# Twenty-four loads moved from ScalarE's queue to GpSimd's in a two-block convolution kernel

## The chip, the cores and the metric

The kernel runs on one core of a Trainium2 chip. The metric is the device time of one execution in microseconds (us). TensorE (PE) multiplies matrices, its weight loads are shown as PEld, VectorE is DVE, ScalarE is ACT, GpSimd is POOL, SyncE is SP. SP, ACT and POOL can each ask for DMA transfers; the instruction that asks is called the issue here.

## What is computed

Two residual blocks on x of shape (8, 96, 96, 192), all in float32:

```
x = x + L0(groupnorm(x))
x = x + L1(groupnorm(x))
...
# L1, the ConvNeXt-like block
y = conv_general_dilated(x, dw_kernel 7x7, SAME, feature_group_count=192) + dw_bias
y = (y - mean_c) * rsqrt(var_c + 1e-6) * ln_gamma + ln_beta
y = gelu(y @ w0 + b0)          # 192 -> 768
y = (y @ w1 + b1) * gamma      # 768 -> 192
```

L0 projects 192 channels to 384, convolves them 3x3 per channel, adds four running averages along rows and columns, normalizes and projects back. Only L1's 7x7 convolution and what surrounds it matter here.

## The kernel before

The work is staged. Stages A to C compute block L0 and leave its result x1 in DRAM as X1_d. Stage D is the 7x7 convolution; stage E ("the last pass") takes the convolution's output back from DRAM (Y_d), normalizes each pixel over the channels, runs the two dense layers and stores the result.

**Stage D** has 32 steps: two halves of the batch (four images each) times 16 groups of 12 channels. A step is one call pattern of conv_d: six sub-steps c, each with two PSUM banks, 24 matmuls (L1337) and two evictions on ScalarE (L1347) that write the step's output tile yo. The first N1 = 19 steps, numbered n = 0 to 18, are the stage's "own steps": they run by themselves in the loop that the diff touches (L1622). The other 13 are later mixed into stage E in slots. In each own step the program order is, engine by engine:

- POOL: load_raw(n + 2) asks for the rows of the step after next, six transfers of 384 KB (L926). Each waits until VectorE has scaled the rows two steps earlier (L960) out of the same buffer.
- SP: load_band(n + 2), one transfer of 624 KB (L936), then store_d(n - 1), the output of the step before: for each of two channel groups one transfer of 810 KB (L1364) and two of 27 KB (L1368, L1369).
- DVE: scale_steps(n + 1) normalizes the rows of the next step into xin (24 instructions, L960), and copies its band to the other half of the partitions (L964).
- PE and ACT: conv_d(n, c) for c = 0 to 5. Before its first eviction, yo must be free: yo has one buffer for even and one for odd steps, so the stores of step n - 2 must have landed.

The order of the instructions is as the program has it (manual_schedule); nothing reorders them afterwards. Eight PSUM banks stand between TensorE and ScalarE, so TensorE can be four sub-steps ahead.

**Tile 0 of the last pass.** Stage E works through tiles; load_y(n) gathers one from Y_d into two SBUF tiles ya and yb. It gives a list of steps: begin (allocates, L1387), then for each image b and for b = NH (the remainder) eight pieces q. A large piece (L1398) reads 32 rows by 5 channel groups in runs of 384 bytes, 60 KB in all, from one part of Y_d, called a chunk: five groups of six channels, that is, the output of two and a half convolution steps. A small piece (L1404) is 16 KB. Since Y_d is filled in the order of the groups, tile 0's large pieces can be asked for while stage D is still running. main_y lists which, by step: chunks 0 and 1 in step 12 (NI = 16, so NI - 4), chunks 2 and 3 in step 13, and chunk 4 (twice) in step 14. These are 8 pieces in each of three steps; they are asked for two after each of the first four sub-steps. The rest, chunk 5 and the small pieces, follows in step 16 from SP and POOL (rest_y), and tile 1 in step 17.

Each piece is a lambda whose engine is an argument with a default; main_y's loop passes the engine.

After the loop, VectorE sums tile 0 over the channels (L1486, norm_steps_e) and the chain to the first dense layer (L1549) begins.

## Time and profile before

| what | value |
|---|---|
| median of 3 runs | 5425.03 us (5417.93 to 5442.97) |
| the profiled execution | 5427.67 us |
| its span, first to last instruction | 5425.9 us |
| TensorE busy | 5255.3 us, 97% |
| VectorE, ScalarE, GpSimd busy | 64%, 48%, 44% |
| own steps of stage D in the span | about 2590 to 2907 us |
| large pieces asked for by ACT | 24, from 2798.8 to 2852.6 us |

Times inside the profile count from the span's start. A line of the waits reads: waiter and its line <- whom it waited for: total us, times, longest us. A line of a timeline reads: start, duration, engine, line, operation, tiles, count, and in brackets the idle time before it with what ended it. A queue line of the DMA view reads: queue and kind: packets, MB, share of the time of 16 DMA engines. q0 is POOL's queue, q1 SP's, q10 ACT's.

### The profile page before, as it was taken

How to read it: one execution, taken by the hardware profiler on the slowest of the kernel's cores; microseconds unless marked ns; L12 is line 12 of the kernel's file. 1: busy time of each engine (PE TensorE's matmuls, PEld its weight loads, DVE VectorE, ACT ScalarE, POOL GpSimd, SP SyncE). 2: the span in 40 equal slices, each digit the busy share in tenths (PEclk: the TensorE clock that was granted, in tenths of full speed). 3: DMA queues.
4: the chain of work that ended last, by engine and by line, in shares of the span. 5: the costliest groups of instructions: out<-in, count | busy, mean ns of one | idle time of the engine just before them, and what ended most of it. 6: DMA issues, size and time to landing. Idle time of an engine off the chain costs nothing. (4 is left out here: it accounts for less than half of the span.)

```text
span 5425.9 us, 107893 instructions
## 1 busy us (share of the span) xinstructions
PE 5255.3 (97%) x42206; PEld 3342.3 (62%) x42206; DVE 3460.8 (64%) x6722; ACT 2578.2 (48%) x5765; POOL 2386.7 (44%) x2105
## 2 busy tenths in 40 slices
PE   6999999999999999999787999999999999999999
PEld 4666643333333799999444666666666667666667
DVE  6555539999999555555556555555566666666654
ACT  2444446777777566565434444454433333323332
POOL 1111118888888555555324222233233333333332
PEclk9999979999999999999898999999999999999999
DMA  7999868999999799899997455545433233332331
GB/s 221 286 286 276 251 181 235 244 246 242 247 241 250 226 306 308 276 303 311 293 299 205 119 137 136 132 120 138 108 80 78 80 81 84 87 93 80 81 78 41
DMA packets 788107, 1015.33 MB, mean 187 GB/s; under 512 B 326199, under 2 KB 662272, under 8 KB 785552
## 3 DMA queue, kind: packets, MB, share of 16 engines
q1 hardware_dynamic: 671432, 633.30, 44.2%
q0 software_dynamic: 86128, 335.43, 18.7%
q10 hardware_dynamic: 30040, 39.72, 3.2%
q8 instruction: 334, 5.47, 0.4%
q14 instruction: 173, 1.42, 0.1%
HBM read 603.70 MB, written 420.03 MB: 189 GB/s over the span
## 5 line engine op out<-in xcount | busy, mean ns | idle before, releaser
L1579 PEld LDWEIGHTS hp<-w1g,g 128*128 128x128 f32 x6912 | 1117.9, 190 | 140.7 <-issue 82.8
L1579 PE MATMUL hp<-w1g,g 128*128 128x192 f32 x6912 | 1174.9, 329 | 0.0
L1568 ACT ACTIVATE g<-hp,b0g 128x512 f32<-128x512 f32 x864 | 518.9, 691 | 1216.1 <-PE hp L1559 1192.9
L1598 POOL DMA_DIRECT2D out_dram<-xo x288 | 211.3, 734 | 1532.5 <-DVE xo L1590 1461.6
L1590 DVE TENSOR_TENSOR xo<-hp,r 128x384 f32<-128x384 f32 x288 | 229.0, 795 | 995.2 <-PE hp L1579 994.9
L1549 PE MATMUL hp<-yT,w0w 128*128 128x512 f32 x1728 | 779.3, 597 | 19.9 <-DVE yT L1534 19.3
L1141 PE MATMUL po<-wc,mt 128*128 128x193 f32 x3456 | 666.4, 328 | 7.5 <-DVE x1c L1175 7.3
L688 PE MATMUL pl<-pin,band 34*32 34x380 f32 (+1 forms) x13824 | 639.0, 496 | 6.4 <-DMA pin<-PL_d 4.2
L775 POOL TENSOR_TENSOR mo<-mo,z 128x768 f32<-128x768 f32 x285 | 593.9, 2084 | 5.7 <-ACT mo L713 1.6
L1141 PEld LDWEIGHTS po<-wc,mt 128*128 128x128 f32 x3456 | 556.0, 192 | 8.9 <-DVE x1c L1175 8.3
L1549 PEld LDWEIGHTS hp<-yT,w0w 128*128 128x128 f32 x1728 | 321.2, 190 | 380.3 <-issue 350.2
L721 DVE TENSOR_TENSOR_SCAN z<-decay,loc 128x768 f32<-128x768 f32 x288 | 505.9, 1757 | 63.7 <-ACT loc L697 34.6
L730 DVE TENSOR_TENSOR_SCAN z<-decay,z 128x768 f32<-128x768 f32 x288 | 498.3, 1730 | 0.0
L1337 PE MATMUL hp<-xin,band 63*64 63x372 f32 (+1 forms) x4608 | 417.9, 498 | 69.3 <-ACT yo L1347 37.3
L688 PEld LDWEIGHTS pl<-pin,band 34*32 34x32 f32 x13824 | 233.7, 108 | 393.5 <-issue 390.9
L709 PE MATMUL pa<-loc,mix 128*32 128x384 f32 x3456 | 439.3, 500 | 0.0
L712 PE MATMUL pa<-last,down 96*32 96x384 f32 x1152 | 434.2, 500 | 0.9 <-ACT mo L713 0.9
L1559 PE MATMUL hp<-yT,w0w 64*128 64x512 f32 x1728 | 419.5, 611 | 0.0
L1513 POOL TENSOR_TENSOR rs<-tot,neg_half 32x32 f32<-32x32 f32 x72 | 394.7, 5481 | 48.2 <-DVE tot L1511 47.4
L1347 ACT ACTIVATE yo<-hp,dwb 128x384 f32<-128x384 f32 x384 | 196.5, 583 | 430.5 <-PE hp L1337 268.1
L697 ACT COPY loc<-pl 128x384 f32<-128x384 f32 x576 | 248.0, 482 | 313.1 <-PE pl L688 313.1
L395 PE MATMUL pm<-xT,win 128*128 128x384 f32 x1152 | 391.9, 490 | 0.0
(159 smaller groups left out, 7261.6 us busy)
## 6 DMA issues: line engine op xcount, KB each, us to landing
P<-po POOLq DMA_DIRECT2D x96, 1152.0 KB, 9.4
pin<-P SPq DMA_DIRECT2D x190, 576.0 KB
mt<-M SPq DMA_DIRECT2D x192, 384.0 KB
xq<-in_x_dram SPq DMA_DIRECT2D x96, 576.0 KB
xr<-in_x_dram SPq DMA_DIRECT2D x192, 288.0 KB
X<-x1c SPq DMA_DIRECT2D x144, 384.0 KB
out_dram<-xo POOLq DMA_DIRECT2D x288, 192.0 KB, 2.4
r<-X SPq DMA_DIRECT2D x35, 1536.0 KB
```

Source lines behind the costliest of these rows:

```text
L688: nc.tensor.matmul(pls[g][at * RB : (at + 1) * RB, :, lo:hi], band[rows, c, kh, :], pin[rows, c, :, NJ - 1 - j, lo + kh - 1 : hi + kh - 1] ...
L709: nc.tensor.matmul(pa[at], mix[:, i, at], loc[:, q], start=True, stop=True)
L712: nc.tensor.matmul(pa[at], down[:, to], last[:, q], start=True, stop=True)
L721: nc.vector.tensor_tensor_scan(zf, decay_f, loc.rearrange("p q n -> p (q n)"), 0.0, ALU.mult, ALU.add)
L730: nc.vector.tensor_tensor_scan(zr, decay_f, zr, 0.0, ALU.mult, ALU.add)
L775: eng.tensor_tensor(m, m, z, ALU.add)
L1141: nc.tensor.matmul(po, mt[:, m, j * 128 : (j + 1) * 128], wc[:, m], start=(m == 0), stop=(m == NC - 1),)
L1337: nc.tensor.matmul(pys[g][k * 64 : (k + 1) * 64, :, lo:hi], band[rows, k * GS + c, d * ZS : d * ZS + 64], xin[rows, :, :, k * GS + c, lo + ...
L1549: nc.tensor.matmul(hps[m, q], w0w[:, 0, m * 128 : (m + 1) * 128], yT[:, 2 * q], start=True, stop=False,)
L1559: nc.tensor.matmul(hps[m, q], w0w[p, 1, m * 128 : (m + 1) * 128], yT[p, 1], start=False, stop=True,)
L1568: nc.scalar.activation(g[:, m, q], hps[m, q], AF.Gelu, bias=b0g[:, m : m + 1], scale=1.0)
L1579: nc.tensor.matmul(po[:, q], g[:, m, q, k * 128 : (k + 1) * 128], w1g[:, m], start=(m == 0), stop=(m == NE - 1),)
```

## The change

In the loop of the own steps the large pieces of main_y are given to GpSimd in place of ScalarE. Nothing else is edited: the same 24 pieces, in the same steps, at the same places in the program. On ACT they stood between the evictions of a step; on POOL they stand behind the six row loads that load_raw(n + 2) has put there earlier in the same step, and ahead of those of load_raw(n + 3).

```
                 for c in range(GS):
                     conv_d(n, c)
                     for step in main_y.get(n, [])[2 * c : 2 * c + 2]:
-                        step(nc.scalar)
+                        step(nc.gpsimd)
                     if c == 2:
                         for step in between:
                             step()
```

More of the change, by code (lines that the diff above doesn't have):

```diff
@@ L1649, in conv_blocks_kernel @@
                     for step in main_y.get(n, [])[2 * c : 2 * c + 2]:
-                        step(nc.scalar)
+                        step(nc.gpsimd)
                     if c == 2:
```

## The prediction

> **What bounds the kernel now.** I went from the page to the stretch that the edit touches. The slices come first, each 135.6 us wide; the edit lies in the 21st and 22nd.

> ```profile
> PE   6999999999999999999787999999999999999999
> DMA  7999868999999799899997455545433233332331
> GB/s 221 286 286 276 251 181 235 244 246 242 247 241 250 226 306 308 276 303 311 293 299 205 119 137 136 132 120 138 108 80 78 80 81 84 87 93 80 81 78 41
> ```

> TensorE is full nearly everywhere (9) and falls to 7 and 8 only in slices 20 to 22. From slice 23 on it is full again, so a microsecond saved in the own steps of the 7x7 convolution is one saved at the end: all that follows hangs on that convolution's results and is TensorE-bound. Next, who waited for whom between 2590 and 2920 us (total, times, longest):

> ```profile
> POOL raw L926 <- DVE xin L960: 169.2, 38, 28.1
> ACT yo L1347 <- DMA Y<-yo: 126.5, 15, 28.4
> ...
> ACT yo L1347 <- DMA ya<-Y: 24.3, 7, 6.2
> ...
> ACT yo L1347 <- DMA yb<-Y: 6.1, 1, 6.1
> ```

> The evictions wait mostly for the stores of the same yo buffer two steps earlier, not for TensorE. Only 24.3 + 6.1 = 30.4 us are waits behind the pieces. The timeline of ScalarE at step 12, the first with pieces (start, duration, [idle before]):

> ```profile
> 2798.74 0.58 ACT L1347 ACTIVATE yo<-hp,dwb 128x384 f32<-128x384 f32 x1 [11.97 <-DMA Y<-yo]
> ...
> 2802.32 5.43 ACTq L1398 DMA_DIRECT2D ya<-Y  x2
> 2807.80 1.05 ACT L1347 ACTIVATE yo<-hp,dwb 128x384 f32<-128x384 f32 x2 [6.09 <-DMA ya<-Y]
> 2809.97 3.50 ACTq L1398 DMA_DIRECT2D ya<-Y  x2
> 2813.53 1.99 ACT L1347 ACTIVATE yo<-hp,dwb 128x384 f32<-128x384 f32 x4 [4.67 <-DMA ya<-Y]
> 2821.70 0.58 ACT L1347 ACTIVATE yo<-hp,dwb 128x384 f32<-128x384 f32 x1 [6.18 <-DMA Y<-yo]
> ```

> The twelve evictions of step 12 last from 2798.74 to 2815.5, 16.8 us; those of step 11 ran from 2778.31 to 2786.76, 8.5 us. The same timeline gives the starts: step 3 at 2664.05 and step 11 at 2778.31, so 14.28 us a step; then 2798.74, 2821.70, 2841.87, 2864.85 (step 15), 2875.89, 2885.79. The three steps with pieces take 23.0, 20.2 and 23.0 us. SyncE's timeline shows a second effect:

> ```profile
> 2786.79 0.33 SPq L1364 DMA_DIRECT2D Y<-yo  x1
> 2797.94 0.26 SPq L1368 DMA_DIRECT2D Y<-yo  x1
> 2798.65 0.26 SPq L1369 DMA_DIRECT2D Y<-yo  x1
> 2807.90 0.33 SPq L1364 DMA_DIRECT2D Y<-yo  x1
> ```

> ```profile
> q0 software_dynamic: 5208, 18.34, 50.5%
> q1 hardware_dynamic: 5674, 18.58, 49.9%
> ```

> ```profile
> q0 software_dynamic: 2443, 8.59, 48.8%
> q1 hardware_dynamic: 2117, 6.96, 35.2%
> q10 hardware_dynamic: 4209, 1.47, 10.2%
> ```

> The ordinary steps are bound by the DMA engines: 100.4% busy. In steps 12 to 14 they are still 94% busy. That limits what the edit can give.

> [...]

> **The change part by part.**

> *Removed from ScalarE:* 24 issues, and the 30.4 us of waits with them. The evictions of steps 12 to 14 should last 8.5 us each instead of 16.8, 12.9 (2821.70 to 2834.55) and 14.7 (2841.87 to 2856.55): 18.9 us in sum, on the path only as far as the stores can follow.

> *Removed from the shared semaphores:* the pattern of SP returns to that of steps 3 to 11, and the late store (about 10 us in each of three steps) goes. It overlaps the item above, so the two aren't added.

> *What is late next: the DMA engines.* The bytes stay. At the rates of steps 3 to 11 (18.34 MB in 57.6 us, 18.58 in 56.9: 0.318 and 0.326 MB/us) the traffic of 2798 to 2865 needs 8.59/0.318 + 6.96/0.326 + 6.8 (the pieces' own 10.2% of 67 us) = 55.2 us. That is 11.8 us less than the 67 taken. If the slow rate came from the mixture itself, only the idle share comes back: 5.2% of 67, 3.5 us. So 3.5 to 12 us by step 15. Steps 15 to 17 ran 82% busy, and rows that come later fill them: -3 to +6 us. I take 8 + 3 = 11 us.

> *Added to GpSimd:* eight issues a step at 0.57 us (its median on L1398), 4.6 us beside rows of 4.4 us in steps of 20 us. Their issue time is hidden by GpSimd's wait for L960 (169.2 us in all). The waits that they bring are not free: after six rows, the last six of eight pieces each look back to one of these rows, so the last piece waits until the rows have landed, and the next step's rows stand behind it. A row lands after

> ```profile
> raw<-X POOLq DMA_DIRECT2D x18, 384.0 KB, 12.9
> ```

> 12.9 us (median, steps 12 to 14), 13.1 us in ordinary steps, 18.2 us at most. With L for this and 4.6 us for issuing six rows, a turn of GpSimd is 5.6 + L, some 19 us. Rows 15 then start at about 2798 (rows 14 went out by 2784, plus L) instead of 2788.45, rows 17 two turns later, and rows 18, whose third looks back to the first of rows 17, are complete at 2798 + 2(5.6 + L) + 0.6 + L + 2.5 + L = 2812 + 4L. Before, VectorE took rows 18 at 2883.43. With L = 13.5 they are there at 2866, 17 us earlier: an 11 us gain fits. The break-even is L = 17.9. The chunk of step 14's pieces holds output of step 12; its store, issued by about 2808, must have landed. GpSimd reaches them near 2820: a cost of 0, at most 3 us. Data for tile 0 come earlier or as late as before, well ahead of VectorE's first sum at 2892.15.

> Sum: 5427.67 us (the profiled execution; span 5425.9) - 11 = 5416.7. It stood 2.6 us above the median of 5425.03, so I forecast **5414 us**.

> **The rivals.**
> *Full recovery.* Steps 12 to 14 fall to 14.28 us plus 2.3 us each for the pieces (6.8/3): 49.7 instead of 66.1 us, 16.4 us, and step 12 and the tail give some 8 more. For it: the late store vanishes completely. Against it: 94% busy engines. 5425 - 24 = 5401.
> *Hidden anyway.* ScalarE, free of the pieces, waits at L1347 for the store instead, since only 3.5 us of the engines' time was idle, and later rows take those back. For it: 126.5 us of that wait already. 5425 - 2 = 5423.
> *Slower: rows behind pieces.* GpSimd's turn becomes the bound. From L = 17.9 us each further microsecond costs four. The most seen is 18.2. With the stores busy without pause and half the rate left for the rows, six of them (2.36 MB) take 2.36/0.163 = 14.5 us, so it needs a further disturbance[...]. At L = 21: 4 x 3.1 = 12 us, 5437; at L = 25 it would be 28 us, 5453.

> **How the numbers follow.** The forecast 0.58, full recovery 0.14, hidden 0.19, slower 0.09. A measurement of this kernel can tell about 0.5% (27 us) from no change; the runs shown spread from 5417.93 to 5442.97. Faster by more needs the upper end of full recovery: 0.06. Slower by more needs L near 25: 0.03. Within: 0.91. The range 5399 to 5430 takes in the 3.5 to 18 us of the forecast, most of full recovery, all of "hidden", and leaves out most of "slower".

> **What would show it.** Right: no idle of L1347 put down to ya or yb, twelve evictions in 8.5 us in steps 12 to 14, the second L1364 of a step a few us after its first, DMA near 100% and some 330 GB/s from 2798 on, starts of steps 13 to 15 some 15 to 18 us apart, TensorE's last L1337 of step 18 some 11 us before 2907.1. Wrong: VectorE (L960) waiting for raw in steps 15 to 17 says GpSimd's turn is the bound; starts still 20 us or more apart with L1347 waiting for Y<-yo says the transfers were.

## The result and the profile after

The changed kernel takes 5410.21 us (median of 21 runs, 5404.86 to 5434.75); the kernel before, on the same chip, 5428.17 us (21 runs). The ratio is 0.9971, 95% interval 0.9962 to 0.9979: some 16 us less, a small gain, but one that the runs can tell from nothing. The forecast was 5414 us.

A caution on the trace: the profiled execution of the changed kernel took 5428.47 us, 18 us above its median; its own steps began late (step 3 at 2666.6 us instead of 2664.05, step 11 at 2783.07 instead of 2778.31) ahead of the first moved piece at 2790.78, in code that the edit doesn't touch, and step 12 began at 2806.05 instead of 2798.74. So I compare stretches inside the stage, not spans, and give the same stretches of the repeat run (label after_again, 5412.05 us) beside them.

The slices of the changed kernel hardly differ from those of before: in the 21st the DMA engines stay at 9, in the 22nd they go from 7 to 8; a few us in a slice of 135.7 us hardly show.

```profile
PE   6999999999999999999787999999999999999999
DMA  7999869999999799899998455545433233332331
GB/s 221 285 286 277 251 183 239 247 240 244 246 243 246 230 306 308 273 301 312 282 308 206 119 137 135 131 120 138 108 79 78 80 81 85 87 92 80 81 78 41
```

The waits of the changed kernel between 2590 and 2920 us (total, times, longest):

```profile
POOL raw L926 <- DVE xin L960: 115.9, 27, 28.1
ACT yo L1347 <- DMA Y<-yo: 112.2, 11, 30.2
...
DVE xin L960 <- DMA raw<-X: 26.4, 8, 8.3
...
POOL ya L1398 <- DMA raw<-X: 19.8, 12, 3.2
```

GpSimd waits less for VectorE (169.2 us before), since part of its time now goes into waiting for its own earlier transfers (the last line, 19.8 us). The third line is new: VectorE waits for rows. Before there was no such wait. ScalarE's timeline from step 12 to step 15:

```profile
2806.05 3.88 ACT L1347 ACTIVATE yo<-hp,dwb 128x384 f32<-128x384 f32 x8 [12.51 <-DMA Y<-yo]
...
2817.18 2.00 ACT L1347 ACTIVATE yo<-hp,dwb 128x384 f32<-128x384 f32 x4 [2.17 <-DMA Y<-yo]
...
2833.31 4.83 ACT L1347 ACTIVATE yo<-hp,dwb 128x384 f32<-128x384 f32 x10 [6.92 <-DMA Y<-yo]
...
2849.57 3.88 ACT L1347 ACTIVATE yo<-hp,dwb 128x384 f32<-128x384 f32 x8 [10.05 <-DMA Y<-yo]
```

These are the starts of steps 12 to 15: 11.1, 16.1 and 16.3 us apart, instead of 23.0, 20.2 and 23.0. Between them no wait is put down to ya or yb. The late second store is gone as well; SyncE's timeline, the pairs of large stores of steps 12 and 13:

```profile
2815.04 0.33 SPq L1364 DMA_DIRECT2D Y<-yo  x1
...
2816.16 0.33 SPq L1364 DMA_DIRECT2D Y<-yo  x1
...
2826.41 0.48 SPq L1364 DMA_DIRECT2D Y<-yo  x1
...
2830.08 0.76 SPq L1364 DMA_DIRECT2D Y<-yo  x1
```

The DMA engines, from the start of step 12 to the start of step 15. First the kernel before (66.1 us; the third line counts rows asked for), then the changed kernel (43.5 us):

```profile
DMA packets 8716, 16.86 MB, mean 255 GB/s; under 512 B 4788, under 2 KB 5130, under 8 KB 8548
...
raw<-X POOLq DMA_DIRECT2D x18, 384.0 KB, 12.9
```

```profile
DMA packets 3986, 12.91 MB, mean 297 GB/s; under 512 B 683, under 2 KB 874, under 8 KB 3788
...
q1 hardware_dynamic: 2144, 7.17, 51.6%
q0 software_dynamic: 1837, 5.67, 48.7%
...
raw<-X POOLq DMA_DIRECT2D x12, 384.0 KB, 13.1
```

That is the picture in two numbers. The same three steps went by 22.6 us faster, but with 3.95 MB less moved: 12 row transfers instead of 18, and 8 of the 24 pieces outside the stretch, since GpSimd had asked for them before step 12 began. Most of what wasn't moved comes next. From the start of step 15 to VectorE's first sum (L1486) the kernel before moved 6.43 MB in 27.3 us, the changed one this:

```profile
DMA packets 4477, 9.89 MB, mean 266 GB/s; under 512 B 1905, under 2 KB 2193, under 8 KB 4410
...
raw<-X POOLq DMA_DIRECT2D x12, 384.0 KB, 16.1
```

It took 37.2 us, 9.9 us more, for 3.46 MB more; the other 0.49 MB are the eight early pieces. From step 12 to the first sum together: 93.4 us before, 80.7 us after (79.6 in the repeat), so 12.7 (13.8) us less. From the start of step 11, ahead of the first piece in both kernels, it is 10.1 (15.8) us less.

| us | steps 3 to 11, each | 12 to 15 | 15 to first sum | 11 to first sum | 3 to first L1549 |
|---|---|---|---|---|---|
| before | 14.28 | 66.1 | 27.3 | 113.8 | 262.3 |
| after | 14.56 | 43.5 | 37.2 | 103.7 | 255.8 |
| after_again | 14.58 | 42.2 | 37.4 | 98.0 | 250.4 |

The widest stretch shows the least, 6.5 and 11.9 us: in both profiles the eight steps from 3 to 11 took over 2 us longer than before, and the way from the first sum to L1549 1.4 us longer. These are single executions; the gain itself is read from the 21 runs.

### The profile page after: what moved, and what is told of

Its sections match the earlier page's. It is cut to its first block, busy times and chain, and to the rows that moved or that the text cites. A ratio compares the mean times of both kernels' runs of the same rounds, so it can differ in the third digit from the quotient of the medians.

```text
span 5426.5 us, 107918 instructions
## 1 busy us (share of the span) xinstructions
PE 5247.6 (97%) x42206; PEld 3346.3 (62%) x42206; DVE 3455.9 (64%) x6722; ACT 2581.9 (48%) x5765; POOL 2405.4 (44%) x2129
## 2 busy tenths in 40 slices
PE   6999999999999999999787999999999999999999
## 3 DMA queue, kind: packets, MB, share of 16 engines
q0 software_dynamic: 86896, 336.90, 18.9%
## 5 line engine op out<-in xcount | busy, mean ns | idle before, releaser
L1549 PE MATMUL hp<-yT,w0w 128*128 128x512 f32 x1728 | 779.2, 597 | 22.1 <-DVE yT L1534 21.9
L1549 PEld LDWEIGHTS hp<-yT,w0w 128*128 128x128 f32 x1728 | 321.2, 190 | 382.3 <-issue 350.5
L1337 PE MATMUL hp<-xin,band 63*64 63x372 f32 (+1 forms) x4608 | 412.7, 496 | 70.9 <-ACT yo L1347 26.9
L1347 ACT ACTIVATE yo<-hp,dwb 128x384 f32<-128x384 f32 x384 | 197.1, 585 | 423.4 <-PE hp L1337 290.2
## 6 DMA issues: line engine op xcount, KB each, us to landing
mt<-M SPq DMA_DIRECT2D x192, 384.0 KB
X<-x1c SPq DMA_DIRECT2D x144, 384.0 KB
```

Source lines behind the costliest of these rows:

```text
L1337: nc.tensor.matmul(pys[g][k * 64 : (k + 1) * 64, :, lo:hi], band[rows, k * GS + c, d * ZS : d * ZS + 64], xin[rows, :, :, k * GS + c, lo + ...
L1549: nc.tensor.matmul(hps[m, q], w0w[:, 0, m * 128 : (m + 1) * 128], yT[:, 2 * q], start=True, stop=False,)
```

## The experiments

Theory: on ScalarE's queue the pieces cost more than their own transfer, through the waits that they bring into its queue (30.4 us of waits at L1347 before; look-back to a transfer eight places earlier) and through a slower mixture of transfers; on GpSimd these waits fall on rows, which have slack. Rivals: it is only the interruption of the evictions; it is only the late second store; or the pieces' transfer itself, wherever it is asked for. Ratios are to the kernel before in the same set of runs, with 95% intervals.

The look-back can be read in the trace's records of the issues, between 2590 and 2880 us of the kernel before. The 149 issues of SyncE and ScalarE signal eight semaphores, numbered 100 and 102 to 108, and can be merged into one order in which these come in turn; GpSimd's signal eight others, 111 to 118, in turn. The two pieces of the 5.43 us bar went out at 2802.32 and 2807.44, 0.31 us each, and the second first waits for semaphore 100, which the piece of 2798.79 signals. Likewise the late second store (2807.90) waits for 108, that of the first (2786.79).

**The changed kernel again** (no edit).

> The changed kernel once more, for a second profile and a comparison on the same chip as the runs beside it. Both theories: some 15 to 18 us below the kernel before. The theory that rows behind pieces are the new bound expects VectorE (L960) to wait for raw in the steps that scale rows 16 and 17 again, by 20 us or more in sum; the theory that only the DMA engines bind expects little of that wait, and the evictions waiting for Y<-yo instead.

Measured: 5412.05 us, 0.9981 (0.9970 to 0.9992). The gain repeats, between 0.1 and 0.3%. VectorE waits 20.7 us for rows again, as the theory of rows behind pieces expected.

**The pieces on SyncE**, kernel before with

```
-                        step(nc.scalar)
+                        step()
```

> The 24 pieces on SyncE in place of ScalarE, at the same places. If the cost was that ScalarE stood still between evictions, this is as fast as the change: some 15 us below before, steps 12 to 14 with evictions of 8.5 us. If the cost was that pieces share the queue and the eight semaphores of the stores, it gains little or loses: -3 to +15 us against before, with the second L1364 of a step still 10 us or more behind the first.

Measured: 5425.72 us, 1.0001 (0.9991 to 1.0012). Nothing is gained, although the evictions are undisturbed (8.3, 6.2 and 7.9 us). Eight pieces hold SyncE's queue instead, with the stores behind them:

```profile
2802.80 14.79 SPq L1398 DMA_DIRECT2D ya<-Y  x8
...
2818.25 0.54 SPq L1364 DMA_DIRECT2D Y<-yo  x1
...
2830.11 15.15 SPq L1398 DMA_DIRECT2D ya<-Y  x8
...
2845.92 0.54 SPq L1364 DMA_DIRECT2D Y<-yo  x1
```

So "off ScalarE" is not what gains; "onto GpSimd" is. And no third queue is needed for the loss: here only two have work in steps 12 to 15, which take 59.3 us at 262 GB/s.

**The pieces on ScalarE, but behind all six sub-steps**, kernel before with

```
-                    for step in main_y.get(n, [])[2 * c : 2 * c + 2]:
-                        step(nc.scalar)
...
+                for step in main_y.get(n, []):
+                    step(nc.scalar)
```

> The pieces stay on ScalarE, but all eight stand behind the twelve evictions of their step. The evictions of a step are then never interrupted, and semaphores stay shared. If interrupted evictions were the cost: some 10 us below before. If the waits of the pieces for stores were (they now stand ahead of the next step's evictions): no gain, -3 to +10 us against before.

Measured: 5431.01 us, 1.0005 (0.9993 to 1.0017). The evictions of steps 12 to 14 take 8.6, 8.0 and 7.9 us, and steps 12 to 15 still 67.8 us. The timeline of ScalarE says where the wait went:

```profile
2819.20 13.23 ACTq L1398 DMA_DIRECT2D ya<-Y  x7
2832.55 3.88 ACT L1347 ACTIVATE yo<-hp,dwb 128x384 f32<-128x384 f32 x8 [13.14 <-DMA ya<-Y]
```

From between the evictions it moved ahead of the next step's first. So the loss needs no interruption between the evictions of a step; that a piece waits in the queue of whoever asks for it is not refuted. The DMA engines of this run, steps 12 to 15, are full and slow all the same:

```profile
DMA packets 9058, 18.67 MB, mean 275 GB/s; under 512 B 4650, under 2 KB 5031, under 8 KB 8853
...
q0 software_dynamic: 2637, 9.22, 51.0%
q1 hardware_dynamic: 2425, 7.99, 38.6%
q10 hardware_dynamic: 3991, 1.39, 10.7%
```

**The two large stores first**, kernel before; the large ones of both groups ahead of the four small ones:

```
-        for k in range(2):
+        for large, k in ((True, 0), (True, 1), (False, 0), (False, 1)):
...
+            if large:
                 nc.sync.dma_start(
...
+                continue
```

> The kernel before with the two large stores of a step ahead of its four small ones, so that the second large store no longer looks back to the first; the pieces stay on ScalarE between evictions. If the late second store was the main cost, 8 to 15 us below before. If the stops of ScalarE were, 0 to 3 us below, or slower, since its sixth and seventh piece now look back to the band and the first large store.

Measured: 5430.89 us, 1.0007 (0.9994 to 1.0020); steps 12 to 15 took 64.2 us. Once the pieces begin, both large stores of a step go out one right behind the other (three pairs, whose bars together take 6.8, 1.0 and 1.1 us), and nothing is gained. But the lateness only moved: now the four small stores come late, those of step 11 behind its second large one as follows.

```profile
2790.68 0.33 SPq L1365 DMA_DIRECT2D Y<-yo  x1
2799.73 0.28 SPq L1370 DMA_DIRECT2D Y<-yo  x1
...
2805.91 0.31 SPq L1371 DMA_DIRECT2D Y<-yo  x1
```

The last of the six goes out 26.4 us behind the step's last eviction, where it was 25.9 us before (2812.66 against 2786.76). Since yo is free only when all six have landed, the run shows that the second large store's place is not the cause; whether the late end of the stores is, it doesn't test.

**More work on ScalarE**, the changed kernel plus three Square instructions of 1024 elements a step behind sub-steps 0 to 2 of steps 12 to 14 (work that the reference doesn't have, into a scratch tile):

```
+                    if n in main_y and c < 3:
+                        busy = sp.tile([128, NH, WE + HV, CK], F32, tag="sq", name="sq", bufs=1)
+                        nc.scalar.activation(..., AF.Square)
```

> The change with three extra Square instructions of 1024 elements on ScalarE, some 2.0 us each, one after each of the first three sub-steps in steps 12 to 14; they write a buffer that nothing reads. The evictions are stretched by some 6 us a step, as they were before on average, with no semaphore shared. If stretched evictions by themselves are on the path: 10 to 18 us above the change, back to 5420 to 5428. If rows and DMA engines bind instead: 0 to 5 us above it.

Measured: 5409.24 us, 0.9968 (0.9958 to 0.9978), steps 12 to 15 in 43.5 us. The Squares took 1.05 us each, half of what was expected, and the evictions of a step 8.6 to 8.7 us. So some 3 us more work a step on ScalarE costs nothing; the stretch of the evictions to 13 to 17 us, as before, was not reproduced.

**Without the 24 pieces** (they are left out, and ya and yb filled with zeros, so tile 0 lacks its data):

```
-                    for step in main_y.get(n, [])[2 * c : 2 * c + 2]:
-                        step(nc.scalar)
...
+                if n == NI - 5:
+                    nc.gpsimd.memset(ya[0], 0.0)
+                    nc.gpsimd.memset(yb[0], 0.0)
```

> The 24 large pieces are left out; tile 0's buffers are filled with zeros by GpSimd instead, so that tile 0's output is not the reference's. This is the ceiling for any way of asking for them. If the DMA engines bind the steps, it lies 6 to 9 us below the change (the pieces' 6.8 us of the 16 engines); if the wait of rows behind pieces costs more than that, 12 to 20 us below it.

Measured: 5398.01 us, 0.9953 (0.9934 to 0.9971). All that pieces can cost is thus some 25 us on ScalarE (0.47% of 5427; by the interval 16 to 36) and 12 to 14 us on GpSimd (5410.21 and the repeat's 5412.05 less 5398.01, with intervals that overlap). That is the second expectation, more than the engines' time alone, for transfers that took 10.4% of the engines' time in 66.1 us before, 6.9 us. The mean rate of steps 12 to 15, 43.9 us, is the highest of all:

```profile
DMA packets 4280, 14.67 MB, mean 334 GB/s; under 512 B 549, under 2 KB 846, under 8 KB 4076
```

**The pieces spread out**, two in each of eight steps (5 to 8, 10 to 13) and four in steps 14 and 15 (ya and yb are allocated in step 4 for it), on GpSimd and on ScalarE:

```
-                NI - 4: [y_0[1 + b * 8 + q] for q in (0, 1) for b in range(NH)],
...
+            for at, q, bs in (
+                (5, 0, (0, 1)), (6, 0, (2, 3)), (7, 1, (0, 1)), (8, 1, (2, 3)),
+                (10, 2, (0, 1)), (11, 2, (2, 3)), (12, 3, (0, 1)), (13, 3, (2, 3)),
+                (14, 4, range(NH)), (15, 6, range(NH)),
+            ):
+                main_y[at] = [y_0[1 + b * 8 + q] for b in bs]
```

> As the change, but the pieces are spread over more steps, each chunk as soon as its stores can have landed: two a step in steps 5 to 8 and 10 to 13, four in steps 14 and 15. With two behind six rows no piece looks back to rows of its own step, with four only the last two do. If rows behind pieces are the change's new bound, VectorE waits little for raw, and the time falls 4 to 8 us below the change (5402 to 5407 us). If the DMA engines bind, the same bytes take the same time: within 3 us of the change.

> The same spread, asked for by ScalarE between evictions as before. If it was the number of pieces per step that hurt on ScalarE (its waits and the shared semaphores), spreading alone recovers most: 8 to 15 us below before. If any piece between evictions costs a stop, 24 pieces cost about what they did before: 0 to 5 us below it.

Measured: on GpSimd 5410.51 us, 0.9966 (0.9957 to 0.9975); on ScalarE 5418.27 us, 0.9979 (0.9969 to 0.9988). With four pieces at most in a step, VectorE never waits for rows in the spread kernel on GpSimd, and step 15 to the first sum takes 29.1 us, not 37.2. Yet its time is that of the changed kernel: steps 12 to 15 take 46.4 us, and steps 3 to 11, where a part of the pieces now lies, 14.62 us each. Putting rows off costs nothing that the runs can tell; it moves time from one stretch to the next. On ScalarE, spreading alone brings 0.21 of the 0.34%, as expected if the number of pieces per step is what hurts. What is left between ScalarE and GpSimd, 0.13%, isn't clear of noise: the two intervals overlap.

**The look-back without the bytes**, the changed kernel plus 24 loads of 4 bytes on ScalarE in the pieces' old places (beyond what the reference needs):

```
+                    if n in main_y and c < 4:
+                        for k in range(2):
+                            at = 8 * (n - NI + 4) + 2 * c + k
+                            nc.scalar.dma_start(tiny[:, at : at + 1], b0[at : at + 1].unsqueeze(0))
```

> The changed kernel, its pieces on GpSimd, with 24 loads of 4 bytes added to ScalarE in steps 12 to 14, two behind each of the first four sub-steps: they take the pieces' places in the shared semaphores and move next to nothing. Theory A (the look-back through the shared semaphores makes a step wait for the stores of the step before): the time goes back towards that of the kernel before, 5418 to 5430 us; steps 12 to 15 take 55 us or more (43.5 and 42.2 in the changed kernel, 66.1 before) and SyncE's queue has under 42% of the engines there (52 after, 35 before). Theory B (it is the pieces' bytes or their landing on ScalarE's queue that hold the evictions): 5407 to 5414 us, steps 12 to 15 within 3 us of 43.5 us. In between, 48 to 53 us, each has a share.

Measured: 5416.48 us, 0.9986 (0.9976 to 0.9996); steps 12 to 15 in 47.6 us. The bars of these loads on ScalarE's queue sum to 22.3 us, as long as those of the pieces before (20.8 us), and the evictions of steps 12 to 14 are stretched to 9.6, 13.8 and 17.1 us (16.8, 12.9 and 14.7 before). One step of them:

```profile
2830.30 8.29 ACTq L1655 DMA_DIRECT2D tiny<-in_L_conv_b_dram  x2
2838.64 0.58 ACT L1347 ACTIVATE yo<-hp,dwb 128x384 f32<-128x384 f32 x1 [9.18 <-DMA Y<-yo]
```

But the time lies between the two: by the medians 6 us of some 18 came back, and the intervals admit from nothing (against the repeat run's 0.9981) to most of it. Step 12 to 15 met neither expectation, 55 us nor within 3 us of 43.5. SyncE's queue keeps its share (48.6% of the engines), so waits of this length alone don't starve it. Theory A as I wrote it falls; it is at most a part.

**The sixth chunk's pieces on GpSimd too**, in the changed kernel and in the spread one:

```
-                NI: [y_0[1 + b * 8 + q] for q in (5, 7) for b in range(NH)]
+                NI: [
+                    lambda s=y_0[1 + b * 8 + q]: s(nc.gpsimd) for q in (5, 7) for b in range(NH)
+                ]
```

> The changed kernel with the eight pieces of the sixth chunk, behind step 16, asked for by GpSimd as well and not by SyncE, where they stand ahead of the stores of step 16. If these stores are what gives back some 10 us behind step 15: 5398 to 5405 us, and step 15 to the first sum falls from 37.3 to 32 us or less. If it is rows 17 and 18 that land late behind the pieces of steps 13 and 14: 5408 to 5414 us, and step 15 to the first sum stays above 35 us.

> The spread pieces (two a step in eight steps, four in each of two) on GpSimd, and those of the sixth chunk behind step 16 there too. No rows stand behind the pieces here, so only the stores of step 16 are freed: if they matter by themselves, 5402 to 5407 us (spread alone 5410.51) and step 15 to the first sum under 27 us; if the DMA engines' own time is what is left, 5408 to 5413 us.

Measured: 5408.90 us, 0.9968 (0.9956 to 0.9979), and 5407.38 us, 0.9968 (0.9956 to 0.9980); step 15 to the first sum took 41.3 and 33.8 us. Neither can be told from the changed kernel, so the pieces ahead of step 16's stores are not what holds the tail. In the first of them VectorE still waits 28.4 us for rows, and step 16 to 17 takes 24.4 us; in the two spread kernels on GpSimd there is no such wait, and the same step takes 7.1 us, or 11.6 with the sixth chunk on GpSimd. So the rows behind the pieces stretch the tail. No version that does all of the work beats the changed kernel by more than its interval.

## Why the prediction was right, and which terms were not

The total was right: 11 us forecast below the profiled execution, 12.7 and 13.8 us less between step 12 and the first sum, 16 us by the ratio (11 to 21 by its interval, 4 to 16 by that of the repeat). Part of that is luck: the 8 us were picked inside "3.5 to 12" without a reason, and two steps that were wrong, the bytes and the pieces' own price, don't show in the sum. (Its own range is 3.5 - 3 to 12 + 6, 0.5 to 18 us, not 3.5 to 18.) Of the signs that I had named, the starts were 11.1, 16.1 and 16.3 us apart, not 15 to 18; the engines were near 100% busy, but at 297 GB/s (308 in the repeat), not 330; and TensorE's last L1337 of step 18 ended 5.1 us (18.7) before 2907.1, on both sides of 11. Point by point:

**ScalarE's evictions, 8.5 us:** right. They took 9.0, 9.2 and 6.2 us. I put them "on the path only as far as the stores can follow"; evictions undisturbed at no gain (5431.01 us with the pieces at the step's end, 5425.72 us with them on SyncE) confirm that caution.

**The late second store:** right that it goes: in steps 11 to 13 it went out 21.1, 16.0 and 16.3 us behind the first before, 5.9, 1.1 and 3.7 us after. Against the 3.2 us of step 5 it had been 13 to 18 us late, not "about 10". Whether its going was worth anything by itself no run shows, since with the large stores put together the small ones were late in its place.

**The DMA engines, 8 us by step 15 and 3 us in the tail:** the sum holds, the split doesn't. Step 15 came 22.6 us nearer to step 12, and 9.9 us were given back after it. The step that failed is "the bytes stay": I priced the stretch as if the same traffic had to be done by step 15. 3.95 MB lay outside it, 3.46 behind and 0.49 ahead, at 297 GB/s 13.3 us. What is left is a change of rate: the 16.86 MB of before at 297 instead of 255 GB/s take 56.8 us, 9.3 us less than 66.1. That is the term that I took at 8, between 3.5 and 12. Likewise in the tail: its rate rose from 236 to 266 GB/s, so its 9.89 MB took 37.2 us instead of 41.9, a gain of 4.7 where I had 3.

**Which end of "3.5 to 12":** "if the slow rate came from the mixture itself, only the idle share comes back". Both came back, idle time and rate. From the start of step 11 to the first sum these kernels moved nearly the same bytes; before, then after, then with the pieces on ScalarE at the step's end:

```profile
DMA packets 13898, 29.55 MB, mean 259 GB/s; under 512 B 6745, under 2 KB 7357, under 8 KB 13503
q1 hardware_dynamic: 5954, 15.57, 46.6%
q0 software_dynamic: 3709, 12.35, 39.9%
q10 hardware_dynamic: 4224, 1.48, 6.0%
```

```profile
DMA packets 10501, 29.78 MB, mean 287 GB/s; under 512 B 2904, under 2 KB 3511, under 8 KB 10107
q0 software_dynamic: 4489, 13.93, 49.2%
q1 hardware_dynamic: 6002, 15.70, 49.2%
```

```profile
DMA packets 13915, 29.66 MB, mean 254 GB/s; under 512 B 6741, under 2 KB 7353, under 8 KB 13523
q1 hardware_dynamic: 5925, 15.49, 46.4%
q0 software_dynamic: 3756, 12.55, 39.7%
q10 hardware_dynamic: 4224, 1.48, 6.5%
```

With the engines' instruction queues (under 1%) they were 93% busy before and 99% after. Their idle time fell from 7.8 us of 113.8 to 1.0 of 103.7, so 6.8 of the 10.1 us are idle time and 3.3 a faster rate (in the repeat 7.3 and 8.5 of 15.8). With the pieces at the end of the step on ScalarE, the engines were 100% busy as far as step 15, but behind it only 68%: over the whole, 93% again. The slow rate isn't tied to a third queue: with the pieces on SyncE it was 253 GB/s over the same stretch, and with the pieces spread out on ScalarE, three queues, 289.

The same 24 pieces from three issuers gave 5425.7 (SyncE), 5427 (ScalarE) and 5410 us (GpSimd): at eight pieces a step, who asks for them is worth some 16 us. In steps 12 to 15 GpSimd's queue had 48.8% of the engines and SyncE's 34.9 with the pieces on ScalarE; with the pieces on GpSimd 48.7, pieces and all, and SyncE's 51.6. With the pieces on SyncE the two had 49.4 and 45.7, SyncE's pieces and all. From these shares I'd estimate that pieces on ScalarE or SyncE take from the stores, while on GpSimd they come out of the rows' half; no run shows this by itself.

**The pieces' own 6.8 us:** taken over unchanged, and this was wrong. The issuer also changes the packets, as the fences above show: on ScalarE's queue the pieces were 4224 packets, and on GpSimd's the whole execution has only 768 more than before (86896 against 86128), with 3840 fewer under 512 bytes. In the trace's records these are 3840 packets of 384 bytes on ScalarE and 384 packets of 3840 bytes on GpSimd, the rest small ones of 4 bytes; the former took 6.6 us of the 16 engines, the latter 4.9 us. On SyncE they are small packets too: from step 11 to the first sum 6708 were under 512 bytes, 6745 before and 2904 after.

**GpSimd's turn, 5.6 + L:** the form was right and the size a little low. The six-row groups of the changed kernel on GpSimd's timeline:

```profile
2806.70 3.69 POOL L926 DMA_DIRECT2D raw<-X  x6
...
2826.74 3.72 POOL L926 DMA_DIRECT2D raw<-X  x6
...
2851.26 5.13 POOL L926 DMA_DIRECT2D raw<-X  x7
```

The turns are 20.0 and 24.5 us, not 19.1: a piece adds its own look-back, at most 5.71 us, and L rose to 16.1 us in the tail. So rows 18 were there at 2882.9, not at 2866; 7 us of this is the late start of this execution. VectorE took them as they came:

```profile
2862.72 2.41 DVE L960 TENSOR_SCALAR xin<-raw,s 128x192 f32<-128x192 f32 x8 [8.31 <-DMA raw<-X]
2869.00 2.41 DVE L960 TENSOR_SCALAR xin<-raw,s 128x192 f32<-128x192 f32 x8 [3.88 <-DMA raw<-X]
```

This is the sign that I had named for "GpSimd's turn is the bound". For steps 16 and 17 it was: step 16 to 17 took 22.8 us, and 7.1 us in the spread kernel. In the end it cost nothing measurable (5410.21 us with that wait, 5410.51 us in the spread kernel without it), and the engines stayed 95% busy from step 15 to the first sum.

**The rivals.** "Full recovery" described the steps (its 49.7 us against 43.5 measured) and not the total: it too took the bytes for constant. "Hidden anyway" is refuted by 0.9962 to 0.9979, and "slower" by the same interval, though its mechanism was at work and some 2 us from its break-even (L = 16.1 of 17.9 by the median; one row took 20.5 us).

**What stays open:** which of at least three things that changed together made the 16 us. The first is the waits that pieces bring into the queues of ScalarE and SyncE; the 4-byte loads, which also bring part of the second, give these at about a third, with an interval from nothing to most. The second is the late end of a step's stores, which would free yo late. The last of the six went out behind the last eviction of steps 11 to 14 by so much:

| us | step 11 | step 12 | step 13 | step 14 | ratio |
|---|---|---|---|---|---|
| before | 25.9 | 16.8 | 18.4 | 13.2 | 1 |
| large stores first | 26.4 | 17.4 | 23.7 | 19.3 | 1.0007 |
| on ScalarE, at the step's end | 9.6 | 20.7 | 17.4 | 22.3 | 1.0005 |
| on SyncE | 9.7 | 18.5 | 29.2 | 21.0 | 1.0001 |
| 4-byte loads | 18.6 | 14.7 | 13.8 | 6.9 | 0.9986 |
| spread, on ScalarE | 14.3 | 10.4 | 19.8 | 17.5 | 0.9979 |
| spread, on GpSimd | 10.5 | 6.6 | 7.5 | 9.9 | 0.9966 |
| after | 11.8 | 1.9 | 7.0 | 9.1 | 0.9971 |

The four kernels without a gain have the latest stores in sum, the two between lie between, the two fastest have the earliest: this goes with the time, in one profile of each, but no run changed it alone. The third is the packets: every run with the pieces on ScalarE or SyncE had the small ones, every run with them on GpSimd the large ones. Spread out on ScalarE, small packets still kept 0.21 of the 0.34%, so they aren't the whole. Not tried: the pieces on ScalarE without its shared semaphores, or in other packets.

## What to carry to other kernels

Where DMA engines bound a stage, ask in whose queue a transfer waits, and what share of the engines each queue then has (SyncE's, with the stores, had 34.9% here with the pieces on ScalarE, 51.6% with them on GpSimd): give it to the issuer whose own transfers have slack (here rows asked for two steps ahead), not to the one that feeds the loop of stores and buffers, and try fewer at a time first, which here brought 0.21 of 0.34% without another issuer. When you read the gain of a stretch, count its bytes and its idle time, and go on until both have come in; a stretch that got faster by moving less has only borrowed the time, and one that is fully busy may have put its idle time off. And a stall that vanishes with the change isn't thereby its cause: evictions left in peace and the last pieces' place each moved the time by nothing. Nor is a cause refuted before the trace shows that the experiment took it away: the reordered stores ended as late as before.

## What the hardware showed unexpectedly

- Busy engines are not fast engines: at 100% busy the same stage ran at 275 GB/s (pieces on ScalarE at the step's end), 297 to 308 (on GpSimd) and 334 (left out).
- 1.47 MB in runs of 384 bytes, 6.9 us of the engines' recorded time, cost some 25 us of the kernel's time from ScalarE's queue and 12 to 14 from GpSimd's.
- The issuer changed the packets: the same pieces were 3840 packets of 384 bytes from ScalarE (6.6 us of the engines) and 384 of 3840 bytes from GpSimd (4.9 us); from SyncE they were small too (6708 packets under 512 bytes from step 11 to the first sum, 6745 from ScalarE).
- In steps 12 to 15 of the changed kernel two queues with work shared the engines nearly evenly (51.6 and 48.7%, 53.0 and 47.7% in the repeat).
